# A two-layer graph kernel on one core: earlier weight sums, second-level pieces in half sets, and one block's left and right evicted whole

## The chip, the cores and the metric

The kernel runs on one core of one Trainium2 chip. A core has five engines, each with its own stream of instructions: TensorE (PE in the profile; its weight loads are PEld), VectorE (DVE), ScalarE (ACT), GpSimd (POOL) and SyncE (SP, which here only issues DMAs). An engine takes its instructions in order; semaphores tie the streams together. The metric is the device time of one execution in microseconds (us), given as the median of several runs.

## What is computed

The input `x` is 128 graphs of 64 nodes with 768 features, all in float32, and `adj` a 64 x 64 adjacency for each graph. Two layers follow each other:

```python
# layer 0: graph attention with left, self and right weights
u = softmax(h @ h.T / sqrt(d));  delta = u * adj
attn = delta / (sum(delta, 2) + 1e-10)
h_left, h_self, h_right = h @ Wl.T + bl, h @ Ws.T + bs, h @ Wr.T + br
ctx = triu(attn, 1) @ h_left + diag(attn) * h_self + tril(attn, -1) @ h_right
x = layernorm(x + relu(norm(ctx) * gamma + beta))
# layer 1: attention with 12 heads of 64
q, k, v = (x @ W + b for W, b in ((Wq, bq), (Wk, bk), (Wv, bv)))
scores = q @ k.T / 8 + abeta * adj, and -9e15 where adj <= 0
x = layernorm(x + softmax(scores) @ v)
```

## The kernel before

The 8192 rows are worked in 16 blocks of 512 rows (four tiles of 128 rows, each tile two graphs). Blocks 0 and 1 of layer 0 come before the main loop. Turn `n` of the loop then does layer 0 of block `m = n + 1` and layer 1 of block `n`, in this order on TensorE: left part, right part, own part (`self_part`) of block `m`, `values` of block `n`, and two `projected` groups (queries and keys) of block `n`. In the code the hooks of these parts are named `left`, `right`, `own`, `val`, `qk[0]` and `qk[1]`; a hook with place `k` is called ahead of product `k` of that part.

**Fewer products.** A matrix product is split into quarters and done with seven products of sums instead of eight (`seven`, `by_tokens`; `ORDER` is the order of the seven, each with two halves of the rows). An `u` eviction (L582) keeps an intermediate sum, and `last` adds the product to it on VectorE. From block `DEEP = 3` on, left and right are done together and each of the seven products is split once more into seven (`both_sides`, `nested`, 49 products); the weights of this second level lie in the DRAM tensor `lr_d`. Layer 1 does its products with fifteen sums (`products`, `FIFTEEN`).

**Weight sums.** All of these schemes need sums of weight quarters, made once. `prepare` makes the first-level sums `t5, t6, 7, t4` of a weight (tiles `b_s`, `t_s`, `b_l`, `t_l`, `b_r`, `t_r`) and stores them to `d_s`, `d_l`, `d_r`. `prepare1` makes 15 sums of the 9 raw ninths of the q, k or v weights: `loaded` issues raw loads on ScalarE's queue (L271), `summed` adds on VectorE (L304, L306), `stored` writes to `v_d` or `qk_d` from POOL's queue (L278 and after). Each raw or summed piece needs a free buffer, a "home"; homes for v are the slots of `xT` and of `x1` (`homes_of_v`). `deepened(i)` makes the second-level pieces of the left and right weights: it loads four `w_deep` tiles on SyncE's queue, copies five quarters from `d_l`/`d_r` to `lr_d`, makes eight subtractions of 128 x 192 on VectorE (L389; four for left and four for right) and stores four results (L395). The tiles `w_deep` come from the same pool of 12 buffers as the streamed weights (`wqk`, `wv`, `wlr`).

**Left and right of a block.** `ctx` needs, in one tile, the left rows of one graph above the right rows of the other (the tile `lr`, with TensorE's transposed attention beside it). Blocks 0 to 2 go by `side_part`, whose `last` evicts each bank of 128 rows in two pieces of 64 rows (L803), each to its place. Later blocks are evicted whole, and `swapped` then exchanges the wrong halves by three ScalarE copies of 64 x 768 for each of the four tiles (L854 to L856).

**What sets the order.** From L1257 on the order of instructions is the order in which the program writes them. Everything that is not a product waits in three queues, `first`, `urgent` and `lazy`; after each product `step` takes a few items from their fronts. `settle(key)` empties a queue until no item of that key is left, on the spot. So an item that is put at the front of `urgent` delays all that stands there already. `later(...)` appends; the second-level steps are put at the front:

```python
at(hooks, place + 3, lambda i=i, steps=steps: urgent.extendleft([(("d", i), *f) for f in reversed(steps)]))
```

Layer 1's softmax for head group `m` of block `n` is begun by `scores(n, m)`, which queues in `urgent`: two `largest` (L1056), two `lowered` (the maximum subtracted, L1060), `exponentials` on ScalarE (16 instructions, L1077), several gaps, and two `turn` (32 x 32 transposes on VectorE, L1081). `weighted(n, m)` calls `settle` for them and then multiplies by `v` (L1107). In turn 1, `scores(0, 1)` is hooked at left 1 and `weighted(0, 1)` at right 2.

Of the kernel before, what the change touches and what calls it, by code (L numbers as in the profile page):

```python
# [11 lines left out]
F32 = mybir.dt.float32  # L12
AF = mybir.ActivationFunctionType
ALU = mybir.AluOpType
# [3 lines left out]
P = 128  # L18
B, L, D = 128, 64, 768
# [4 lines left out]
T = 4  # L24
# [46 lines left out]
def gnn_two_layers(ctx: ExitStack, tc, x, adj, wl, bl, ws, bs, wr, br, gamma, beta,  # L71
# [36 lines left out]

    bias_lr = const.tile([P, 2, D], F32, tag="bias_lr", name="bias_lr")
    bias["l"], bias["r"] = bias_lr[:, 0, :], bias_lr[:, 1, :]  # L110
    bias["q"], bias["k"] = column(bq, "bq"), column(bk, "bk")
    abeta_c = const.tile([P, 1], F32, tag="abeta", name="abeta")
    nc.scalar.dma_start(out=abeta_c, in_=abeta.partition_broadcast(P))
    nc.vector.tensor_scalar(abeta_c, abeta_c, SCALE, None, ALU.mult)

    ident = const.tile([P, P], F32, tag="ident", name="ident")
    make_identity(nc, ident)
# [121 lines left out]
    def homes_of_v():  # L239

        xT = tp.tile([P, KC, NTOK], F32, tag="xT", name="h_v")
        yield from (xT[:, c, :] for c in range(KC))
        for t in range(T):
            yield x1_p.tile([P, D], F32, tag="x1", name="h_v")[:, 0 : 2 * TH]
# [124 lines left out]
              *[idle] * waits[2], partial(formed, 4, t4, b[1, 0], t6), queue=queue)  # L369
        return {i: a[0] for i, a in in_sbuf.items()}  # L370

    def deepened(i):


        w = {}

        def begin():
            for j, nm in enumerate("lr"):
                src = pieces[nm][i]
                for k in range(2):  # L380
                    w[j, k] = weight("w_deep").rearrange("p (h c) -> p h c", h=2)
                    nc.sync.dma_start(out=w[j, k], in_=src[:, k, :].rearrange("p (h c) -> p h c", h=2))
                nc.gpsimd.dma_start(out=lr_d[i - 1, 0:3, :, j, :].rearrange("m p c -> p m c"), in_=src[:, :, 0:QUAD])
                nc.gpsimd.dma_start(out=lr_d[i - 1, 3:5, :, j, :].rearrange("m p c -> p m c"), in_=src[:, 1:3, QUAD:HALF])

        def formed(j):
            b11, b12, b21, b22 = (w[j, k][:, h, :] for k in range(2) for h in range(2))
            for out, a, b in ((b11, b12, b11), (b12, b22, b12), (b22, b22, b11), (b21, b21, b22)):
                nc.vector.tensor_tensor(out, a, b, ALU.subtract)  # L389

        def end():
            for j in range(2):
                for k in range(2):
                    d = lr_d[i - 1, 5 + 2 * k : 7 + 2 * k, :, j, :].rearrange("m p c -> p m c")
                    nc.gpsimd.dma_start(out=d, in_=w[j, k])  # L395

        return begin, [(partial(formed, 0),), (partial(formed, 1),), (end, "gap")]

    def transposed(src, xT, t):

# [281 lines left out]
    def loads(n):  # L682

        blocks[n]["xa"] = xa = [xa_p.tile([P, D], F32, tag="xa", name=f"xa_{n}_{t}") for t in range(T)]
        return [partial(nc.sync.dma_start, out=xa[t], in_=x_t[n, t]) for t in range(T)]

    def edges(n):
        blk = blocks[n] = {}
# [91 lines left out]
    class Pairs:  # L780
# [4 lines left out]
        def __getitem__(self, t):  # L785
            if t // 2 not in self.tiles:
                self.tiles[t // 2] = l0t.tile([P, 2, 2, D], F32, tag="lr", name=f"lr_{self.n}_{t // 2}")
            return self.tiles[t // 2][:, t % 2]

    def side_part(n, nm, in_sbuf, hooks={}):  # L790


        blk = blocks[n]
        if nm == "l":
            blk["lr"] = Pairs(n)
        lr = blk["lr"]

        def last(t, h, ps, part):
            cols = slice(h * HALF, (h + 1) * HALF)
            for g in range(2):  # L800
                rows = slice(g * L, (g + 1) * L)
                half = "lr".index(nm)
                recent["u"] = nc.vector.tensor_tensor(lr[t][half * L : (half + 1) * L, g, cols], ps[rows],  # L803
                                                       bias[nm][rows, cols] if part is None else part[rows], ALU.add)

        by_tokens(nm, blk["S"], last, in_sbuf, hooks)

    def both_sides(n, hooks):
# [42 lines left out]
        def swapped(t):  # L851
            low, high = lr[t][0:L, 1, :], lr[t][L:P, 0, :]
            swap = l1s_p.tile([P, T * 6 * L], F32, tag="s", name="swap")
            nc.scalar.copy(swap[0:L, 0:D], high)  # L854
            nc.scalar.copy(high, low)
            nc.scalar.copy(low, swap[0:L, 0:D])  # L856

        return [partial(swapped, t) for t in range(T)]

    def context0(n):  # L860

# [325 lines left out]
    def now(fs):  # L1187
        for f in fs:
            f()

    edges(0)
    homes = [(-1, home) for home in homes_of_v()]
    now(loads(0))
    blocks[0]["rows"] = blocks[0]["xa"]
    in_sbuf = prepare("s", prep, prep)
    bias["s"] = row(bs, "bs")
# [62 lines left out]
    for n in range(NBLK):  # L1259
# [33 lines left out]
        if not last:  # L1293
            if n > 0:
# [229 lines left out]
```

## Time and profile before

| what | us |
|---|---|
| median of 3 runs | 2813.65 |
| the three runs | 2813.05, 2813.65, 2816.16 |
| the profiled execution, whole time | 2813.63 |
| its span in the profile | 2811.9 |
| TensorE busy | 2775.8 |
| VectorE busy | 1951.1 |
| ScalarE busy | 1099.0 |
| POOL busy | 961.5 |

The span runs from the first to the last instruction that the profile shows; some 1.7 us of the time lie around it. Rows of the time line give start, duration, engine, line, operation, output and inputs with their shape, the number of instructions that were merged, and in square brackets the idle time before the row with the one that ended it. Rows of the windows give, for each engine, busy time and instruction count, and at the end the granted TensorE clock (1.00 is full), the share of time in which the DMA engines were busy, and GB/s. Wait rows give the total, the number of times, and the longest.

The stages that the change touches lie in the first 500 us: blocks 0 and 1 until about 207 us, turn 0 of the loop until about 290 us, and turn 1 with block 2's left part from 290, its right part until about 352, its own part until about 382, then values, queries and keys.

### The profile page before, as it was taken

To read this page: it belongs to the slowest core of one execution; us is meant where nothing else is said; L and a number is where in the kernel's file an instruction comes from. 1 tells how busy PE (TensorE), PEld (TensorE's weight loads), DVE (VectorE), ACT (ScalarE), POOL (GpSimd) and SP (SyncE) were. 2 spreads that over 40 slices of the span, in tenths; PEclk is the share of its full clock that TensorE was granted. 3 is DMA by queue.
4 is the path that set the end of the run, shared out by engine and by line. 5 is a ranking of instruction groups with operands and counts; after the bars stand their busy time and mean duration, and the time that the engine had idled before them with its cause. 6 is when DMAs were issued, how large, how long until landed. Compare 5 with 4: busy or idle time off the path is not lost.

```text
span 2811.9 us, 49390 instructions
## 1 busy us (share of the span) xinstructions
PE 2775.8 (99%) x17962; PEld 2014.2 (72%) x17962; DVE 1951.1 (69%) x3412; ACT 1099.0 (39%) x1894; POOL 961.5 (34%) x1251
## 2 busy tenths in 40 slices
PE   8999999999999999999999999999999999999997
PEld 5558677586776867768577685867768677686786
DVE  5787768676685766767677676776767667676666
ACT  0013324335343453434525344353434534345253
POOL 3242234505134151442415225061341513424122
PEclk9999999999999999999999999999999999999999
DMA  9686788857759587695866858678695876948543
GB/s 339 201 294 200 210 259 268 263 157 238 219 181 271 151 258 196 190 269 152 264 184 210 249 169 265 161 230 230 184 262 152 253 204 190 269 147 260 175 128 102
DMA packets 394848, 604.88 MB, mean 215 GB/s; under 512 B 49296, under 2 KB 277648, under 8 KB 394608
## 3 DMA queue, kind: packets, MB, share of 16 engines
q1 hardware_dynamic: 337280, 495.72, 59.3%
q0 software_dynamic: 18704, 76.89, 7.7%
q10 hardware_dynamic: 38624, 29.11, 5.1%
q8 instruction: 146, 2.39, 0.4%
q14 instruction: 94, 0.77, 0.1%
HBM read 530.00 MB, written 78.45 MB: 216 GB/s over the span
## 4 chain that ended last, share of the span: by engine, by line
PE 92%; issue 2%; DMA 2%; DVE 2%; ACT 1%; POOL 0%; SPq 0%; POOLq 0%; ACTq 0%; DVEq 0%
PE ps_X L487 25%; PE ps_Y L487 17%; PE ps_Y L832 13%; PE ps_X L832 11%; PE ps_X L549 10%; PE ps_Y L549 8%; PE ps_ctx L882 3%; PE sc L1044 2%; PE ps_y L1107 2%; PE u L710 1%; PE ps_X L595 1%; ACT eT L1077 1%; DMA b_r<-in_L_gnn_W_right_dram 1%; DMA qk_d<-h_qk 0%; DVE lr L803 0%
## 5 line engine op out<-in xcount | busy, mean ns | idle before, releaser
L435 POOL TENSOR_TENSOR sums<-hT 128x768 f32<-128x768 f32 x16 | 29.7, 1855 | 794.0 <-PE ps_X L487 713.9
L1077 ACT ACTIVATE eT<-s 32x384 f32<-32x384 f32 x512 | 267.1, 522 | 13.8 <-DVE s L1060 7.4
L487 PE MATMUL ps_X<-xT,wqk 128*128 128x256 f32 x1024 | 234.2, 379 | 0.4 <-ACT xT L405 0.4
L893 ACT ACTIVATE unused<-o 128x768 f32<-128x768 f32 x60 | 50.7, 845 | 447.6 <-DMA sq<-in_x_dram 281.2
L617 DVE TENSOR_TENSOR lr<-ps_Y,u_deep 128x384 f32<-128x384 f32 x273 | 151.9, 556 | 94.8 <-PE ps_Y L832 77.0
L1020 ACT ACTIVATE qk<-ps_X,bq 128x256 f32<-128x256 f32 x128 | 60.8, 475 | 395.0 <-PE ps_X L487 394.8
L487 PEld LDWEIGHTS ps_X<-xT,wqk 128*128 128x128 f32 x1024 | 194.5, 190 | 27.0 <-ACT xT L405 0.6
L832 PE MATMUL ps_Y<-wlr,q 128*128 128x384 f32 x546 | 208.5, 491 | 0.0
L1023 DVE TENSOR_TENSOR qk<-qk,ps_X 128x512 f32<-128x512 f32 x160 | 109.7, 686 | 132.1 <-PE ps_X L487 66.9
L1118 POOL TENSOR_TENSOR o<-o,share 128x192 f32<-128x192 f32 x240 | 135.6, 592 | 146.5 <-DVE share L1115 146.4
L487 PE MATMUL ps_Y<-more,wqk 128*128 128x256 f32 x768 | 181.6, 379 | 2.4 <-DMA wqk<-qk_d 1.3
L487 PE MATMUL ps_X<-sums,wqk 128*128 128x256 f32 x768 | 180.3, 381 | 1.1 <-DVE qk L1023 1.1
L465 POOL TENSOR_TENSOR more<-xT 128x512 f32<-128x512 f32 x32 | 40.1, 1273 | 376.9 <-DVE xT L423 198.3
L487 PEld LDWEIGHTS ps_Y<-more,wqk 128*128 128x128 f32 x768 | 145.8, 190 | 22.9 <-DVE d L740 1.7
L487 PEld LDWEIGHTS ps_X<-sums,wqk 128*128 128x128 f32 x768 | 144.6, 190 | 21.5 <-DVE qk L1023 1.5
L1023 DVE TENSOR_TENSOR qk<-qk,ps_Y 128x512 f32<-128x512 f32 x160 | 108.5, 678 | 70.6 <-PE ps_Y L487 68.7
L617 DVE TENSOR_TENSOR u_deep<-ps_X,lr 128x384 f32<-128x384 f32 x195 | 107.8, 553 | 67.0 <-PE ps_X L832 57.9
L549 PE MATMUL ps_X<-ws,hT 128*128 128x384 f32 x462 | 154.0, 486 | 0.0
L832 PE MATMUL ps_X<-wlr,q 128*128 128x384 f32 x364 | 149.2, 492 | 2.3 <-issue 2.3
L832 PEld LDWEIGHTS ps_Y<-wlr,q 128*128 128x128 f32 x546 | 101.5, 190 | 67.3 <-DVE lr L617 0.2
L1158 ACT ACTIVATE unused<-o 128x768 f32<-128x768 f32 x56 | 47.4, 846 | 236.6 <-POOL o L1118 234.0
L549 PEld LDWEIGHTS ps_X<-ws,hT 128*128 128x128 f32 x462 | 87.7, 190 | 61.0 <-DMA ws<-d_s 0.2
(272 smaller groups left out, 6337.4 us busy)
## 6 DMA issues: line engine op xcount, KB each, us to landing
wlr<-lr_d SPq DMA_DIRECT2D x819, 192.0 KB, 3.6
wqk<-qk_d SPq DMA_DIRECT2D x480, 256.0 KB, 2.7
wv<-v_d SPq DMA_DIRECT2D x240, 256.0 KB, 6.1
ws<-d_s SPq DMA_DIRECT2D x180, 192.0 KB, 6.9
ws<-in_L_gnn_W_self_dram SPq DMA_DIRECT2D x135, 192.0 KB, 4.0
xa<-in_x_dram SPq DMA_DIRECT2D x64, 384.0 KB, 5.6
out_dram<-o POOLq DMA_DIRECT2D x60, 384.0 KB, 7.9
sq<-in_x_dram ACTq DMA_DIRECT2D x56, 384.0 KB, 9.3
```

The lines of the kernel that those rows point to most:

```text
L487: nc.tensor.matmul(ps[:, h, :], lhsT=a, rhs=b, start=start and h == 0 and k == 0, stop=k == len(fs[h]) - 1, skip_group_check=True)
L549: nc.tensor.matmul(ps, lhsT=a, rhs=b, start=(c == 0 and i in (1, 2, 5)), stop=(c == len(fs) - 1), skip_group_check=True)
L617: nc.vector.tensor_tensor(dst, view(ps), add, ALU.add)
L832: nc.tensor.matmul(ps, lhsT=a, rhs=b, start=(k == 0 and j in (1, 2, 5)), stop=(k == len(fs) - 1), skip_group_check=True)
L882: nc.tensor.matmul(ps[g * L : (g + 1) * L, 0:HALF], lhsT=blk["aT"][:, t, g * L : (g + 1) * L], rhs=blk["lr"][t][:, g, h * HALF : (h + 1) * ...
L893: nc.scalar.activation(unused(), o[t], AF.Identity, accum_out=total[:, t : t + 1])
L1020: nc.scalar.activation(dst[:, h], ps[:, h, :], AF.Identity, bias=bias["qk"[h]][:, c : c + 1], scale=float(sign))
L1023: nc.vector.tensor_tensor(dst, dst, ps, ALU.add if sign > 0 else ALU.subtract)
L1044: nc.tensor.matmul(sc[t // 2, r][g * L : (g + 1) * L, t % 2, c, :], lhsT=q[rows, c, tok], rhs=k[rows, c, tok], start=True, stop=True)
L1077: nc.scalar.activation(e[to[0], :, to[1]], pairs[rows, :, cols], AF.Exp, scale=1.0 / SCALE)
L1107: nc.tensor.matmul(y[h, r][cols, t, c, :], lhsT=eT[rows, 2 * h + t, c, cols], rhs=by_parity[rows, 2 * h + t, 2 * c + m, g, :], start=True, ...
L1118: nc.gpsimd.tensor_tensor(res, res, share[:, t], ALU.add)
```

## The change

The adjacency of block 0 is loaded behind the four tiles of `x`, and the lines that load `bq`, `bk` and `abeta` stand further down. Three more `prep` tiles (six homes) are put at the front of the homes for the v sums. The sums of the queries begin at place 4 of block 1's own part and those of the keys at place 7 of its left part (both 9 before). `deepened` works on one side, left or right, at a time: two `w_deep` tiles, four subtractions and two stores, in 14 slots instead of seven whole sets. Block 2's left and right are evicted in whole banks of 128 rows, and `swapped` runs for its four tiles at own 1 to 4.

```diff
-    bias["q"], bias["k"] = column(bq, "bq"), column(bk, "bk")
     abeta_c = const.tile([P, 1], F32, tag="abeta", name="abeta")
-    nc.scalar.dma_start(out=abeta_c, in_=abeta.partition_broadcast(P))
-    nc.vector.tensor_scalar(abeta_c, abeta_c, SCALE, None, ALU.mult)
...
-    def deepened(i):
-        w = {}
+    def deepened(i, j):
+        w, src = {}, pieces["lr"[j]][i]
         def begin():
-            for j, nm in enumerate("lr"):
-                src = pieces[nm][i]
-                for k in range(2):
-                    w[j, k] = weight("w_deep").rearrange("p (h c) -> p h c", h=2)
-                    nc.sync.dma_start(out=w[j, k], in_=src[:, k, :].rearrange("p (h c) -> p h c", h=2))
-                nc.gpsimd.dma_start(out=lr_d[i - 1, 0:3, :, j, :].rearrange("m p c -> p m c"), in_=src[:, :, 0:QUAD])
-                nc.gpsimd.dma_start(out=lr_d[i - 1, 3:5, :, j, :].rearrange("m p c -> p m c"), in_=src[:, 1:3, QUAD:HALF])
+            for k in range(2):
+                w[k] = weight("w_deep").rearrange("p (h c) -> p h c", h=2)
+                nc.sync.dma_start(out=w[k], in_=src[:, k, :].rearrange("p (h c) -> p h c", h=2))
+            nc.gpsimd.dma_start(out=lr_d[i - 1, 0:3, :, j, :].rearrange("m p c -> p m c"), in_=src[:, :, 0:QUAD])
+            nc.gpsimd.dma_start(out=lr_d[i - 1, 3:5, :, j, :].rearrange("m p c -> p m c"), in_=src[:, 1:3, QUAD:HALF])
...
-        return begin, [(partial(formed, 0),), (partial(formed, 1),), (end, "gap")]
+        return begin, [(formed,), (end, "gap")]
...
         def last(t, h, ps, part):
             cols = slice(h * HALF, (h + 1) * HALF)
+            if n > 1:
+                recent["u"] = nc.vector.tensor_tensor(lr[t][:, "lr".index(nm), cols], ps,
+                                                      bias[nm][:, cols] if part is None else part, ALU.add)
+                return
             for g in range(2):
...
-    edges(0)
     homes = [(-1, home) for home in homes_of_v()]
+    blocks[0] = {}
     now(loads(0))
+    edges(0)
...
     sides(0)
+    bias["q"], bias["k"] = column(bq, "bq"), column(bk, "bk")
+    nc.scalar.dma_start(out=abeta_c, in_=abeta.partition_broadcast(P))
+    nc.vector.tensor_scalar(abeta_c, abeta_c, SCALE, None, ALU.mult)
     affine_of["gamma"] = row(gamma, "gamma")
     affine_of["beta"] = row(beta, "beta")
     bias["v"] = row(bv, "bv")
+    for _ in range(3):
+        free = prep.tile([P, HC, HALF], F32, tag="w", name="h_v").rearrange("p k c -> p (k c)")
+        homes[0:0] = [(-1, free[:, k * 2 * TH : (k + 1) * 2 * TH]) for k in range(2)]
     prepare1("v", homes)
...
-    self_part(1, None, {9: [partial(prepare1, "q", homes, queue=urgent)]})
-    side_part(1, "l", None, {9: [partial(prepare1, "k", homes, queue=urgent)]})
+    self_part(1, None, {4: [partial(prepare1, "q", homes, queue=urgent)]})
+    side_part(1, "l", None, {7: [partial(prepare1, "k", homes, queue=urgent)]})
...
-        for i, (when, hooks, place) in zip(ORDER2, ((0, val, 2), (0, qk[0], 5), (1, left, 8), (1, own, 3),
-                                                    (1, qk[0], 0), (1, qk[0], 7), (1, qk[1], 3))):
+        slots = ((0, val, 2), (0, val, 7), (0, qk[0], 0), (0, qk[0], 4), (0, qk[0], 8), (0, qk[0], 12), (0, qk[1], 2),
+                 (1, left, 1), (1, left, 4), (1, left, 7), (1, left, 10), (1, qk[0], 0), (1, qk[0], 3), (1, qk[0], 6))
+        for k, (when, hooks, place) in enumerate(slots):
             if when == n:
-                begin, steps = deepened(i)
+                i, j = ORDER2[k // 2], k % 2
+                begin, steps = deepened(i, j)
                 at(hooks, place, begin)
-                at(hooks, place + 3, lambda i=i, steps=steps: urgent.extendleft([(("d", i), *f) for f in reversed(steps)]))
+                more_at = (qk[1], 0) if hooks is qk[0] and place == 12 else (hooks, place + 3)
+                at(*more_at, lambda i=i, steps=steps: urgent.extendleft([(("d", i), *f) for f in reversed(steps)]))
...
                     side_part(m, "l", None, left)
                     side_part(m, "r", None, right)
+                    for t in range(T):
+                        at(own, 1 + t, swapped, blocks[m]["lr"], t)
```

`swapped` is moved out of `both_sides` unchanged, with the tile as an argument.

More of the change, by code (lines that the diff above doesn't have):

```diff
@@ L370, in prepare, with formed @@
         return {i: a[0] for i, a in in_sbuf.items()}
-    def deepened(i):
-        w = {}
+    def deepened(i, j):
+        w, src = {}, pieces["lr"[j]][i]
         def begin():
-            for j, nm in enumerate("lr"):
-                src = pieces[nm][i]
-                for k in range(2):
-                    w[j, k] = weight("w_deep").rearrange("p (h c) -> p h c", h=2)
-                    nc.sync.dma_start(out=w[j, k], in_=src[:, k, :].rearrange("p (h c) -> p h c", h=2))
-                nc.gpsimd.dma_start(out=lr_d[i - 1, 0:3, :, j, :].rearrange("m p c -> p m c"), in_=src[:, :, 0:QUAD])
-                nc.gpsimd.dma_start(out=lr_d[i - 1, 3:5, :, j, :].rearrange("m p c -> p m c"), in_=src[:, 1:3, QUAD:HALF])
-        def formed(j):
-            b11, b12, b21, b22 = (w[j, k][:, h, :] for k in range(2) for h in range(2))
+            for k in range(2):
[3 more added lines that the diff above has]
+            nc.gpsimd.dma_start(out=lr_d[i - 1, 3:5, :, j, :].rearrange("m p c -> p m c"), in_=src[:, 1:3, QUAD:HALF])
+        def formed():
+            b11, b12, b21, b22 = (w[k][:, h, :] for k in range(2) for h in range(2))
             for out, a, b in ((b11, b12, b11), (b12, b22, b12), (b22, b22, b11), (b21, b21, b22)):
@@ L391, in end @@
         def end():
[L392 to L395, printed above, removed]
-        return begin, [(partial(formed, 0),), (partial(formed, 1),), (end, "gap")]
+            for k in range(2):
+                d = lr_d[i - 1, 5 + 2 * k : 7 + 2 * k, :, j, :].rearrange("m p c -> p m c")
+                nc.gpsimd.dma_start(out=d, in_=w[k])
+        return begin, [(formed,), (end, "gap")]
     def transposed(src, xT, t):
@@ L687, in edges @@
     def edges(n):
-        blk = blocks[n] = {}
+        blk = blocks.setdefault(n, {})
         blk["at"] = tmp.tile([P, T, L], F32, tag="adj", name=f"adj_{n}", bufs=3)
@@ L788, in __getitem__, with swapped @@
             return self.tiles[t // 2][:, t % 2]
+    def swapped(lr, t):
+        low, high = lr[t][0:L, 1, :], lr[t][L:P, 0, :]
+        swap = l1s_p.tile([P, T * 6 * L], F32, tag="s", name="swap")
+        nc.scalar.copy(swap[0:L, 0:D], high)
+        nc.scalar.copy(high, low)
+        nc.scalar.copy(low, swap[0:L, 0:D])
     def side_part(n, nm, in_sbuf, hooks={}):
@@ L849, in both_sides @@
                lambda b: bias_lr[:, :, HALF + b * QUAD : HALF + (b + 1) * QUAD], hooks)
[L851 to L858, printed above, removed]
+        return [partial(swapped, lr, t) for t in range(T)]
     def context0(n):
@@ L1189, in now @@
             f()
+    homes = [(-1, home) for home in homes_of_v()]
+    blocks[0] = {}
+    now(loads(0))
     edges(0)
-    homes = [(-1, home) for home in homes_of_v()]
-    now(loads(0))
     blocks[0]["rows"] = blocks[0]["xa"]
```

## The prediction

> **What bounds the kernel now.** I read the page's busy shares, then TensorE's waits, then the time lines of VectorE and ScalarE around each wait, and last the windows with the granted clock.
>
> ```profile
> span 2811.9 us, 49390 instructions
> PE 2775.8 (99%) x17962; PEld 2014.2 (72%) x17962; DVE 1951.1 (69%) x3412; ACT 1099.0 (39%) x1894; POOL 961.5 (34%) x1251
> ...
> PE ps_x L404 <- DMA xa<-in_x_dram: 5.4, 1, 5.4
> PE ps_Y L549 <- DVE lr L803: 3.9, 2, 3.1
> PE ps_X L832 <- issue: 2.3, 1, 2.3
> PE ps_y L1107 <- DVE eT L1081: 1.5, 1, 1.5
> PE sc L1044 <- DVE qk L1023: 1.4, 1, 1.4
> ...
> PE ps_X L487 <- issue: 1.3, 1, 1.3
> PE ps_Y L487 <- DMA wqk<-qk_d: 1.3, 1, 1.3
> ```
>
> TensorE (PE) is busy 99% of the span, so only its idle time can be won, and a new wait of TensorE is lost whole. The wait rows give us in total, times, longest. The matmuls stand in the same order in both built programs, and from about 500 us on the other engines' orders are the same too. There TensorE is busy without a gap until the tail. So the time changes by TensorE's idle time before 500 us, and by the clock after it. Inside that stretch idle is 5.39 at the start, 3.09 at 55.8, about 0.8 near 105, 0.59 and 0.78 at 172 and 177, 1.53 at 325, and 1.30, 1.28, 1.40 and 2.25 at 404, 433, 472 and 478.
>
> **Part 1, loads at the start.** Behind the four x loads, the adjacency load lets the first x land 0.49 us sooner (one issue on the SyncE queue). At 22.60 TensorE takes the first matmul of `t_s,sums`, whose POOL sums hang on the third b_s load (landing at 14.82), not on x, so the half microsecond is waited back. The bq, bk and abeta lines move in the text only: on ScalarE's queue they stay the first three. I take 0 (0 to -0.5).
>
> **Part 2, free homes for the v sums.** Two instead of five raw v loads are issued in the first 20 us, and two stores leave 24 to 27 us: 5 x 256 KB = 1.28 MB less. The wait that this meets:
>
> ```profile
> 57.04 0.56 DVE L355 TENSOR_TENSOR t_r<-b_r 128x384 f32<-128x384 f32 x1 [7.81 <-DMA b_r<-in_L_gnn_W_right_dram]
> 57.63 1.12 DVE L803 TENSOR_TENSOR lr<-ps_Y,u 64x384 f32<-64x384 f32 x2
> ...
> 58.90 3.78 PE L549 MATMUL ps_Y<-t_l,sums 128*128 128x384 f32 x6 [3.09 <-DVE lr L803]
> ...
> 56.00:57.00 1.00, 0.00 (x0) 0.00 (x0) 0.00 (x0) 0.00 (x0) 0.00 (x0) 1.00 1.10 393
> ...
> 59.00:60.00 1.00, 1.00 (x3) 0.56 (x4) 0.97 (x3) 0.00 (x0) 0.36 (x1) 0.66 1.03 389
> 60.00:61.00 1.00, 1.00 (x3) 0.58 (x2) 1.00 (x3) 0.00 (x0) 0.74 (x2) 0.50 0.59 221
> 61.00:62.00 1.00, 1.00 (x3) 0.51 (x2) 1.00 (x3) 0.00 (x0) 0.84 (x2) 0.50 0.77 287
> 62.00:63.00 1.00, 1.00 (x4) 0.56 (x3) 1.00 (x2) 0.00 (x0) 0.77 (x2) 0.64 0.58 215
> ```
>
> VectorE is held 7.81 us by a sum of the right weights, the eviction behind it is late, and TensorE stands 3.09 us. The windows end with granted clock, DMA share and GB/s: DMA is full at 393, so 1.28 MB is 1.28/0.39 = 3.3 us of it, and b_r can land at about 53.7, enough for no stall. After the stall the clock falls: (1-0.66)+0.50+0.50+(1-0.64) = 1.7 us more. The Trainium skill (TensorE: Matmul & The Clock Gate, "Part 1: The HAM clock gate") has the clock halve only after an idle window of about 3.4 us: by it this stall of 3.09 would cost 3.1, by the rows 4.8. The rows decide. (The 2.25 us stall at 478 left the clock at 1.00.) I take -4.0 of 0 to -4.8, since the b_r loads are also gated by TensorE's use of their buffers. The v loads now come when TensorE frees the t_l pieces, near 67 to 70 us, with sums from about 75 on; landings here take 7 to 12 us under full DMA, so they are just in time. Price 0 (0 to +1.5).
>
> **Part 3, q and k sums sooner.** VectorE starts on the q sums at about 134 us instead of 142, and the sums in block 1's right part (each 0.68 to 0.76, as at L306 and L304), which sat before late evictions, thin out. The 0.59 and 0.78 stalls go; VectorE stays tight (83 of 101 us busy from 105 to 206), and one of 0.7 may return. -0.7 (-1.4 to +0.7).
>
> **Part 4, half sets.** The 56 subtractions stay 56; a half set is four of them in a row, 1.45 us. In the first loop turn (207 to 290 us) there are seven half sets against two whole ones: three more, 4.4 us of VectorE beside 17 us of its idle time, and each less than the 3.45 us of two products by which an eviction must be done (a product is 3.45/2 us here): 0 (0 to +2).
>
> The harm is in block 2's left part (290 to 325 us). A half set is pushed to the front of `urgent`, at hooks 4, 7, 10 and 13, once per three products, where before one set came at hook 11. What they push back is the softmax chain of `scores(0, 1)`, in the same queue. Before it ran thus:
>
> ```profile
> 301.16 0.96 DVE L1060 TENSOR_TENSOR s<-s,mx 128x768 f32<-128x768 f32 x1
> 302.14 0.56 DVE L582 TENSOR_TENSOR u<-ps_X,bias_lr 128x384 f32<-128x384 f32 x1
> 302.62 0.95 DVE L1060 TENSOR_TENSOR s<-s,mx 128x768 f32<-128x768 f32 x1
> ...
> 325.21 0.56 DVE L582 TENSOR_TENSOR u<-ps_X,bias_lr 128x384 f32<-128x384 f32 x1 [0.59 <-PE ps_X L549]
> 325.69 1.83 DVE L1081 STREAM_TRANSPOSE eT<-eT 128x768 f32<-128x768 f32 x2
> ...
> 303.67 1.28 ACT L1077 ACT_TABLE_LOAD   x1 [8.78 <-DVE s L1060]
> 304.96 8.54 ACT L1077 ACTIVATE eT<-s 32x384 f32<-32x384 f32 x16
> ...
> 326.71 1.79 PE L1107 MATMUL ps_y<-v,eT 64*64 64x65 f32 x96 [1.53 <-DVE eT L1081]
> ```
>
> The second subtraction of the maximum (302.62) releases ScalarE, whose 16 exponentials end at 313.5, 12 us ahead of the transposes. In the changed program's VectorE order this second subtraction stands behind both u evictions of the right part's product 1 and directly before the two transposes: it is no longer popped step by step, but emptied out by `settle` when `weighted(0, 1)` is written. TensorE's order is unchanged: `weighted(0, 1)` comes at 325.18. Then: eviction 325.21, subtraction 325.69 to 326.64, table load 1.28, exponentials 8.54, first transpose half of 1.83 with 0.1 to start: 326.7 + 1.3 + 8.5 + 1.0 = 337.6 against 326.71: **+10.9 us**, with no cover: VectorE and ScalarE each take their instructions in order, and TensorE has the matmuls behind it. The Trainium skill (ScalarE: Activation LUTs, on what ACT_TABLE_LOAD costs) adds a drain of about 1.38 to the load, 2.66 in all; here the exponentials follow 0.01 us after the 1.28 load, so +10.9, where the page would give +12.3. The stall of 12.5 us also ends cold, as that at 58.9 did: +1.7, together **+12.6**.
>
> **Part 5, block 2 evicted whole.** 32 evictions of 64 rows (0.555 us each at L803) become 16 of 128 rows (0.556, the like row at L582 and L774): 16 x 0.56 = 8.9 us less on VectorE in 290 to 352. That shortens no wait but leaves room for the half sets. ScalarE gets 12 copies of 64x768, 0.83 each by its rows at L854 to L856, 10 us, in 352 to 382, where it is busy 4 of 30 us. Queued behind them are the sq loads (issued at 377.07 before): with the copies done near 368 they lose nothing: 0 (0 to +1).
>
> **Part 6, what follows the stall.** For 11 us TensorE stands while DMA and POOL go on, no set is left in block 2's own part (the 8 subtractions at 365 and their four stores), and the q and k stage of this turn has three half sets instead of three whole ones. The waits there were: sq landing late (VectorE held 4.01 until 403.41; TensorE 1.30), wqk behind the w_deep loads on SyncE (1.28), VectorE's backlog (1.40 and 2.25). All of it is 6.2; I take -4.5 (0 to -6.2).
>
> **Sum.** 0 - 4.0 - 0.7 + 0 + 12.6 + 0 - 4.5 = +3.4 us on the profiled execution, 2813.63 (span 2811.9 and 1.7 around it); the median of three runs is 2813.65, so the same: 2817.0. A measurement of this kernel can tell about 0.2%, 5.6 us, so this counts as within it, on the slow side.
>
> **Rivals.** *A, slower: b_r does not land sooner.* Place: the stall at 55.8. Its third load waits 4.9 us for TensorE and is issued at 46.2 whatever the traffic before. For it: that wait. Against: DMA is full from there to 57. Price: the 4.0 fails, +7.4, 2821.0. It decides from a landing later than 56.2 on: then over 2.25 us of idle are left, and the clock may still fall.
> *B, slower: the waits from 404 to 478 stay* (VectorE is busy 58 of 70 us from 430 to 500): the 4.5 fails, +7.9, 2821.5. With A, +11.9, 2825.5.
> *C, faster: the softmax chain is not late*, because something I have not seen lets the exponentials go early. Then -4.0 - 0.7 - 4.5 = -9.2, 2804.4. Against it is the instruction order itself.
> *D, the change does not do what it says at the start:* the ScalarE queue's order is indeed unchanged; 0.
>
> **How the numbers follow.** The forecast 0.43; A 0.24, B (with and without A) 0.18; C and the like 0.15. The range 2808 to 2826 holds the forecast and most of A and B; left out are C and a tail where all bounds are bad. Faster 0.15, same 0.43, slower 0.42.
>
> **What would show it.** TensorE's waits: `ps_y <- DVE eT` near 12.5 us once, at about 320 to 325 plus what was won, with a table load and 16 exponentials inside, and a clock under 1 after it; no wait for lr at 55.8, b_r landing by 54; none or little at 172 and 177; at most one of the four waits after 400. Wrong, if the exponentials end well ahead of the transposes, if the stall at 55.8 stays, or if a new wait over 1 us shows in 207 to 290 us.

## The result, and the profile after

The changed kernel takes 2826.22 us, the median of 5 runs (2823.75 to 2827.95), against 2816.16 for the kernel before in 5 runs beside it (2813.05 to 2818.98). The ratio is 1.0035, with a 95% interval of 1.0025 to 1.0046: slower, by 10 us. The forecast was 2817.0, in a range of 2808 to 2826, and no difference that can be told. The measured time lies on the slow side, 0.2 us beyond the range.

The page and TensorE's waits (in total, times, longest), of the changed kernel:

```profile
span 2826.2 us, 49392 instructions
PE 2778.6 (98%) x17962; PEld 2015.9 (71%) x17962; DVE 1944.2 (69%) x3396; ACT 1107.1 (39%) x1906; POOL 960.5 (34%) x1251
...
PE ps_y L1105 <- DVE eT L1079: 12.5, 1, 12.5
PE ps_x L398 <- DMA xa<-in_x_dram: 5.8, 3, 4.4
PE ps_X L543 <- DMA wl<-d_l: 2.8, 1, 2.8
PE ps_X L543 <- DVE u L576: 2.3, 2, 2.0
PE ps_Y L543 <- DVE lr L808: 1.6, 2, 0.9
```

The wait for eT of 1.5 us has become 12.5. New are a wait for a `wl` load and one for a `u` eviction; the waits of the 404 to 478 us stretch are gone from the list. The matmuls stand in the same order in all kernels of this study, 17962 of them, so the start of the k-th matmul in one profile less that in another says where time is lost or won. By stage, in us, against the profile of before:

| stage (time before) | forecast | changed kernel | the same once more (`after_again`) |
|---|---|---|---|
| start, to 28 | 0 | +2.6 | +2.7 |
| the wait at 55.8 and the clock after it | -4.0 | -5.0 | -5.0 |
| block 1, 164 to 200 | -0.7 | +3.0 | +2.4 |
| end of turn 0, 283 to 293 | 0 | +1.6 | +1.6 |
| block 2's left part, 312 to 324 | 0 | +3.0 | +2.7 |
| the softmax chain, 324 to 348 | +12.6 | +13.5 | +13.6 |
| 404 and 433 | -4.5, both rows together | -3.1 | -3.1 |
| 472 and 478 | in the row above | -3.8 | -3.8 |
| later | 0 | +1.8 | +0.6 |
| sum | +3.4 | +13.7 | +11.7 |

The two profiled executions are 14.3 us apart and the medians 10.1: the profile of before was one of its quicker executions, that of the changed kernel the slowest of its five. The experiments show which rows are the change's own and which are an execution's luck.

### The profile page after: what moved, and what is told of

It is laid out like the page before. It is cut to its first block, busy times and chain, and to the rows that moved or that the text cites. A ratio compares the mean times of both kernels' runs of the same rounds, so it can differ in the third digit from the quotient of the medians.

```text
span 2826.2 us, 49392 instructions
## 1 busy us (share of the span) xinstructions
PE 2778.6 (98%) x17962; PEld 2015.9 (71%) x17962; DVE 1944.2 (69%) x3396; ACT 1107.1 (39%) x1906; POOL 960.5 (34%) x1251
## 4 chain that ended last, share of the span: by engine, by line
PE 93%; DVE 2%; DMA 2%; ACT 2%; issue 1%; POOL 0%; ACTq 0%; SPq 0%; POOLq 0%
PE ps_X L481 25%; PE ps_Y L481 17%; PE ps_Y L837 13%; PE ps_X L837 10%; PE ps_X L543 10%; PE ps_Y L543 8%; PE ps_ctx L880 3%; PE sc L1042 2%; PE ps_y L1105 2%; PE u L704 2%; ACT eT L1075 1%; PE ps_X L589 1%; DMA bs<-in_L_gnn_b_self_dram 0%; DMA qk_d<-h_qk 0%; DVE lr L808 0%
```

## The experiments

Runs named `b_` are the kernel before with a part of the change; those named `a_` are the changed kernel with an edit.

### Parts of the change alone, on the kernel before

The adjacency behind x:

```diff
-    edges(0)
     homes = [(-1, home) for home in homes_of_v()]
+    blocks[0] = {}
     now(loads(0))
+    edges(0)
```

> The kernel before, with one edit: block 0's adjacency is loaded behind the four tiles of x. In the changed kernel TensorE's first matmul of t_s,sums comes at 25.28 us, 2.6 later than before. Theory: this edit does it (the adjacency's 256-byte rows now go beside the last x tiles and the b_s loads): t_s,sums at 24.5 to 25.5, a stretch of half clock near 11 us, and the whole 1 to 3 us longer. Rival: it comes from the other loads (fewer h_v) or from the scatter of single executions: t_s,sums within 0.5 us of 22.6.

Measured 2815.72 against 2815.07, ratio 1.0002 (0.9994 to 1.0010). The first `t_s,sums` is 1.0 later than before, with no half clock near 11 us: less than the theory had it, more than the rival allowed. In the median the edit by itself costs nothing that can be told, though the interval reaches up to 2.8 us; the theory as stated falls.

The free homes:

```diff
+    for _ in range(3):
+        free = prep.tile([P, HC, HALF], F32, tag="w", name="h_v").rearrange("p k c -> p (k c)")
+        homes[0:0] = [(-1, free[:, k * 2 * TH : (k + 1) * 2 * TH]) for k in range(2)]
     prepare1("v", homes)
```

> The kernel before, with one edit: three more prep tiles as homes for the v sums, so that two instead of five raw v loads and no v store go before 57 us. Theory: the full DMA queue is shorter and b_r lands by 54: no wait for lr at 55.8, no half clock after it, 4 to 5 us less by 62 us. Rival: b_r is held by TensorE's use of its buffers: the wait stays near 3.1. On block 1 (160 to 200 us): if the 3.0 us that the changed kernel lost there come from TensorE running ahead of the k weight's loads, they show here too; if from the sooner q and k sums, not.

Measured 2810.36, ratio 0.9983 (0.9974 to 0.9991): 4.7 us faster. Of the two time lines of VectorE below, the first is of the changed kernel, the second of this one: the first sum of the right weights no longer starts at 57.04.

```profile
54.19 0.56 DVE L352 TENSOR_TENSOR t_r<-b_r 128x384 f32<-128x384 f32 x1 [2.35 <-DMA b_r<-in_L_gnn_W_right_dram]
```

```profile
54.77 0.56 DVE L355 TENSOR_TENSOR t_r<-b_r 128x384 f32<-128x384 f32 x1 [4.48 <-DMA b_r<-in_L_gnn_W_right_dram]
```

It still waits for b_r, but the eviction behind it is in time for TensorE, and the wait of 3.09 and the half clock are gone. In the four profiles without the free homes that wait is not of one size: 3.09 (before), 3.47 (`b_start`), 1.47 (`b_sooner`) and 3.73 (`b_whole`), with half clock behind the first and the last alone. So -5.0 is what the one profile of before had to lose. In block 1 `b_homes` loses 1.0 of the changed kernel's 3.0.

The sooner q and k sums:

```diff
-    self_part(1, None, {9: [partial(prepare1, "q", homes, queue=urgent)]})
-    side_part(1, "l", None, {9: [partial(prepare1, "k", homes, queue=urgent)]})
+    self_part(1, None, {4: [partial(prepare1, "q", homes, queue=urgent)]})
+    side_part(1, "l", None, {7: [partial(prepare1, "k", homes, queue=urgent)]})
```

> The kernel before, with one edit: q sums from place 4 of block 1's own part, k sums from place 7 of its left part. Theory: this is what costs 3.0 us in block 1 of the changed kernel (VectorE waits for a raw k weight's load, 3.1 us near 166): TensorE's idle time in 160 to 200 us goes from 1.4 to 3 or more. Rival: the edit is harmless by itself and takes away the waits of 0.59 and 0.78: idle time there under 1.4.

Measured 2814.69, ratio 0.9997 (0.9989 to 1.0005). Idle time in block 1's right part is 0.66 + 0.69 + 0.89 = 2.2, between the two forecasts. A wait of 0.9 at 185 is this edit's own (every kernel with it has one of 0.88 to 0.92). But kernels without the edit lose time there too against the profile of before: `b_start` 1.4, `b_homes` 1.0, `b_whole` 1.9. Part of the 3.0 is luck of that one profile; more on this at the end of the experiments.

Block 2 evicted whole, with `swapped` at own 1 to 4:

```diff
+            if n > 1:
+                recent["u"] = nc.vector.tensor_tensor(lr[t][:, "lr".index(nm), cols], ps,
+                                                      bias[nm][:, cols] if part is None else part, ALU.add)
+                return
```

> The kernel before, with one edit: block 2's left and right evicted whole, and 12 ScalarE copies in its own part. Forecast: VectorE 9 us less busy in 290 to 352, TensorE's waits there unchanged (1.5 for eT), the sq loads on ScalarE's queue not later: 0 to 1 us by 400 us. Rival: the copies hold the sq loads, and the wait near 405 grows past 2 us.

Run once, 2815.19; the wait for eT is 1.6, and from 200 to 400 us it loses 0.5. As forecast, it costs and brings next to nothing by itself, as far as one execution tells.

### The chain of scores(0, 1)

First the whole of the stall in the changed kernel, from the time lines of VectorE, ScalarE and TensorE:

```profile
330.50 0.56 DVE L576 TENSOR_TENSOR u<-ps_X,bias_lr 128x384 f32<-128x384 f32 x1 [1.38 <-PE ps_X L543]
330.98 0.95 DVE L1058 TENSOR_TENSOR s<-s,mx 128x768 f32<-128x768 f32 x1
341.86 1.84 DVE L1079 STREAM_TRANSPOSE eT<-eT 128x768 f32<-128x768 f32 x2 [9.94 <-ACT eT L1075]
...
325.36 3.78 ACT L929 ACTIVATE o<-o,c,rstd 128x768 f32<-128x768 f32 x4 [31.15 <-DVE c L925]
332.03 1.28 ACT L1075 ACT_TABLE_LOAD   x1 [2.89 <-DVE s L1058]
333.32 8.51 ACT L1075 ACTIVATE eT<-s 32x384 f32<-32x384 f32 x16
...
342.99 2.88 PE L1105 MATMUL ps_y<-v,eT 64*64 64x65 f32 x96 [12.52 <-DVE eT L1079]
```

It is the forecast row by row: the subtraction between the second eviction and the transposes, then 1.28 and 8.51. But ScalarE shows one thing more: four normalisations of block 1 (L929) now stand ahead of the exponentials, held until 325.36 by a factor that VectorE computes late (at 325.18; at 315.74 in `a_slots` below, where two of the half sets stand elsewhere). The test is to put half sets behind the `lowered` only:

```diff
-                at(*more_at, lambda i=i, steps=steps: urgent.extendleft([(("d", i), *f) for f in reversed(steps)]))
+                def more(i=i, steps=steps):
+                    k = 0
+                    while k < len(urgent) and getattr(urgent[k][1], "func", gap).__name__ in ("largest", "lowered"):
+                        k += 1
+                    for f in reversed(steps):
+                        urgent.insert(k, (("d", i), *f))
+
+                at(*more_at, more)
```

> The changed kernel, with one edit: a half set is put behind the two maximum subtractions (lowered) of a softmax chain where these stand at the front of the urgent queue, not ahead of them. VectorE's second subtraction for scores(0, 1) comes back to where it was. Theory: the wait of 12.5 us for eT falls to under 2 and the half clock after it goes: 12 to 13.5 us less near 327 to 350. What follows tells two readings apart: if TensorE's standstill gave the later stages their room, the waits of 1.3, 1.3, 1.4 and 2.3 at 405 to 478 return (whole: about 6 us under the changed kernel); if moving the sets out of block 2's own part did it, they stay away (whole: 12 to 13 us under it, some 2814 or less). A half set now comes later, so w_deep buffers are held longer: the wait for wl at 316 may grow by up to 2 us.

Measured 2822.55, ratio to before 1.0025 (1.0017 to 1.0032). The wait for eT is still 8.7. `lowered` is back at 306.68, and yet on ScalarE's time line:

```profile
327.12 3.78 ACT L929 ACTIVATE o<-o,c,rstd 128x768 f32<-128x768 f32 x4 [30.70 <-DVE c L925]
330.92 1.28 ACT L1075 ACT_TABLE_LOAD   x1
332.22 8.51 ACT L1075 ACTIVATE eT<-s 32x384 f32<-32x384 f32 x16
```

The expectation of under 2 fails: the late subtraction was one of two causes in a row. The exponentials themselves are items of the queue, and half sets ahead of them put them behind the normalisations. (At the end of turn 0 this rule loses 2.7 instead of 1.6.) So they go ahead as well:

```diff
-... in ("largest", "lowered"):
+... in ("largest", "lowered", "exponentials"):
```

> The changed kernel, with half sets put behind the leading lowered and exponentials of a softmax chain in the urgent queue, not ahead of them. With the lowered alone ahead, the exponentials still began only at 330.9, behind four normalisations of block 1 that waited on ScalarE for a VectorE factor until 327. Theory: ScalarE's order is the second half of the cause; with the exponentials ahead too, the wait for eT is under 2 us, as before the change. Rival: w_deep or wl transfers, later by the half set that is pushed back, hold TensorE instead; then 2 us or more of waits for wl in 312 to 328.

Run once, 2814.95: eT 3.1, and waits for `wl` and `wr` of 0.75, 0.52, 0.16 and 0.84, 2.3 together. The theory's "under 2" fails by the subtractions of one half set, which now stand directly before the transposes (329.96 to 331.49 on VectorE); the exponentials themselves are done at 313.98. The rival held as well: the chain is repaired, and weight loads are late instead, by what seems to be the half set that is pushed back and holds its buffers longer. In turn 0 this rule takes away the waits at 283 to 293 entirely (0 against +1.6). Last, the queue as in the change, but the sets elsewhere:

```diff
-                 (1, left, 1), (1, left, 4), (1, left, 7), (1, left, 10), (1, qk[0], 0), ...
+                 (1, left, 7), (1, left, 10), (1, own, 2), (1, own, 5), (1, qk[0], 0), ...
```

> The changed kernel, with the four half sets of block 2's left part put elsewhere: from left 1, 4, 7, 10 to left 7, left 10, own 2, own 5. The second lowered of scores(0, 1) and its exponentials then stand where they stood before the change, on VectorE and on ScalarE. Theory (the chain was late because half sets took its turns in the queue, on both engines): the wait for eT is 1.5 us, no half clock after it, and the whole 12 to 16 us under the changed kernel, 2810 to 2814. Whether the waits of 1.4 and 2.3 at 472 and 478 stay away tells where their gain came from: the standstill of 12.5 us (then they are back, 3.7 us) or the sets that left the last two stages of this turn (then not).

Measured 2814.57, ratio 0.9998 (0.9989 to 1.0007), some 12 us under the changed kernel, and just above the 2810 to 2814 expected. ScalarE and TensorE:

```profile
302.10 1.28 ACT L1075 ACT_TABLE_LOAD   x1 [11.42 <-PE ps_y L1105]
303.39 8.52 ACT L1075 ACTIVATE eT<-s 32x384 f32<-32x384 f32 x16
...
325.52 1.79 PE L1105 MATMUL ps_y<-v,eT 64*64 64x65 f32 x96 [1.62 <-DVE eT L1079]
```

The exponentials end at 311.9, some 13 us ahead of TensorE's need. The wait for `wl` is gone too, and 472 and 478 still cost 3.7 less than before though TensorE stood nowhere: that gain comes from the sets that left the second turn's last stages, not from the standstill.

The wait for `wl` in the changed kernel, on TensorE, and behind it what SyncE's queue waited for in 300 to 330 us:

```profile
318.80 1.56 PE L543 MATMUL ps_X<-wl,hT 128*128 128x384 f32 x4 [2.75 <-DMA wl<-d_l]
...
SPq L570 <- DMA lr_d<-w_deep: 5.4, 4, 2.2
```

Four times a weight load stood still until a half set's result had been stored from the buffer that it needs. With the four half sets as in the change TensorE's wait is 1.9 to 2.8 in three profiles; with two of them (`a_slots`, `best_a`, `best_b` below) or three (`best_c` to `best_e`) it is 0. So their number and place in the left part decide. The queue's waits alone do not: in `a_slots` there are still 5.7 us of them, three times, and TensorE loses nothing. How far the loads run ahead of TensorE was not varied by itself.

### The start

> The changed kernel, with block 0's adjacency loaded first again, ahead of x. Each edit alone (adjacency behind x; fewer early v loads) moved TensorE's first t_s,sums by about 1 us, together by 2.6 to 4.3, where the second t_s sum on VectorE began at 18.2 behind a late b_s load and ran for 4.5 us beside two POOL sums (1.36 us alone). Theory: both are needed to bring b_s late enough; with the adjacency first the sum runs ahead of POOL's at 1.4 us, and t_s,sums is at 22.6 to 24. Rival: the fewer v loads alone do it with the other edits: still at 25 or later.

The edit is that of `b_start` undone. Run once, 2820.40; `t_s,sums` is 1.0 later than before, and the chain as in the changed kernel (12.5). That is in keeping with the theory. The other side of it:

> The kernel before, with the adjacency behind x and the free homes for the v sums, nothing else. In the changed kernel and two of its three variants with both edits the first t_s,sums came at 24.9 to 25.3, in one at 22.5; with one or none of the edits at 22.6 to 24. Theory: the two together make it a race between the second t_s sum and POOL's sums, lost in most executions: some 2 us slower in the median than the free homes alone (2810.4), 2811.5 to 2814. Rival: the start varies from run to run and no edit matters: 2810 to 2811.

Measured 2813.46 (2808.6 to 2819.0), ratio 0.9994 (0.9987 to 1.0001): 3.1 slower than the free homes alone. But its one profile shows the quick start, and at 404 and 433 it loses 4.5 more than theirs: the median cannot be booked on the start.

> The changed kernel once more, beside the others on one chip: 2823 to 2829; a wait of 12.5 us for eT, 2 to 3 us for wl near 315 to 319, none at 472 and 478. If the start is a race, t_s,sums is again near 25 or near 22.5, and nothing between; the 404 and 433 waits, which came and went with no edit near them, may show.

Measured 2825.57, ratio 1.0036 (1.0022 to 1.0049); `t_s,sums` at 25.37. VectorE, then POOL, then TensorE, of this run:

```profile
15.65 1.36 DVE L354 TENSOR_TENSOR t_s<-b_s 128x1152 f32<-128x1152 f32 x1 [4.25 <-DMA b_s<-in_L_gnn_W_self_dram]
18.27 4.55 DVE L354 TENSOR_TENSOR t_s<-b_s,t_s 128x1152 f32<-128x1152 f32 x1 [1.26 <-DMA b_s<-in_L_gnn_W_self_dram]
...
18.02 1.82 POOL L430 TENSOR_TENSOR hT<-hT 128x768 f32<-128x768 f32 x1
19.79 1.81 POOL L441 TENSOR_TENSOR sums<-hT,sums 128x768 f32<-128x768 f32 x1
...
25.37 4.11 PE L543 MATMUL ps_X<-t_s,sums 128*128 128x384 f32 x12 [2.26 <-DVE u L576]
```

and of `a_slots`, whose start has the same edits:

```profile
16.61 1.36 DVE L354 TENSOR_TENSOR t_s<-b_s,t_s 128x1152 f32<-128x1152 f32 x1
...
17.60 2.04 POOL L430 TENSOR_TENSOR hT<-hT 128x768 f32<-128x768 f32 x1
```

If the last b_s quarter lands in time, the second sum is all but done when POOL begins (1.36). If not, it begins beside POOL's two sums and takes 4.55, and the `u` eviction behind it is late: 2.0 to 3.3 us of TensorE, in four of the six profiles of kernels with both edits, in none of the eleven others. The changed kernel and `a_slots` have the same start and differ in this, so it is a race. What makes it losable shows on SyncE's queue, here of before and of the changed kernel:

```profile
3.74 4.17 SPq L233 DMA_DIRECT2D b_s<-in_L_gnn_W_self_dram  x4
...
4.66 5.03 SPq L230 DMA_DIRECT2D b_s<-in_L_gnn_W_self_dram  x4
```

The last of the four b_s loads is issued at 7.2 to 7.8 us in the ten profiles with the adjacency first, and at 8.6 to 9.7 in the seven with it behind x. It lands at 16.15 to 17.09 in the ten, and at 18.05 to 18.19 in the four that lose, while POOL begins at 17.55 to 18.02. So in these profiles it takes the adjacency behind x to lose. Whether the free homes are needed too is not shown: with the adjacency behind x and without them there is one profile (`b_start`), and it won, but so did that of `b_both`.

### Better versions, and the wait at 404

`best_a` is the changed kernel with the adjacency first, the places of `a_slots` and the rule of `a_chain2`; `best_b` leaves out the sooner sums and the whole eviction as well.

> The changed kernel with three edits together: the adjacency first again, the left part's half sets at left 7, left 10, own 2, own 5, and half sets put behind a chain's lowered and exponentials where these stand at the front. Forecast, stage by stage against the kernel before: start 0 to +1, the wait at 55.8 gone (-5), block 1 as before within 1, no wait at 283 to 293, 1.6 for eT at 325, no waits at 472 and 478 (-3.8): about -8, 2805 to 2809. If the -3.8 was bought with the standstill, it is missing here: 2809 to 2812.

> As the version before it, but with the q and k sums at their old places and block 2 evicted in halves, so that only the free homes and the half sets are left of the change. If these two parts are worth nothing by themselves, it is equal to that version within 2 us; if the room on VectorE in block 2 (9 us) or the sooner sums carry part of the gain, it is 2 us or more slower, with waits for lr in 172 to 190 or in 300 to 350.

Measured 2811.65, ratio 0.9985 (0.9979 to 0.9992), and 2810.76, 0.9981 (0.9974 to 0.9988). They are equal within 2 us, as expected, but both some 4 to 5 us short of a forecast of about 2807. `best_a` fell into the range set out for the case that the 3.8 us at 472 and 478 had been bought with the standstill, but by chance: its profile keeps them (-3.7). What is missing lies at 404, where TensorE waited 4.3 and 3.4 us with half clock after it. VectorE and TensorE of `best_b`:

```profile
395.26 0.69 DVE L987 TENSOR_TENSOR v<-v,ps_Y 128x512 f32<-128x512 f32 x1
402.01 1.08 DVE L417 STREAM_TRANSPOSE hT<-sq 128x512 f32<-128x512 f32 x1 [6.07 <-DMA sq<-in_x_dram]
...
403.76 3.51 PE L481 MATMUL ps_X<-wv,more 128*128 128x256 f32 x8 [3.37 <-issue]
```

Two kernels take the sets out of that stretch: `best_c` on `best_b`, `best_d` on `best_a`.

```diff
+        slots = ((0, val, 2), (0, val, 7), (0, val, 11), (0, qk[0], 0), (0, qk[0], 4), (0, qk[0], 8), (0, qk[0], 12),
+                 (0, qk[1], 2), (1, left, 4), (1, left, 7), (1, left, 10), (1, qk[0], 3), (1, qk[0], 6), (1, qk[0], 9))
```

> The free homes and the half sets alone (q and k sums and block 2's eviction as before the change, adjacency first), half sets behind a chain's lowered and exponentials, and other places: eight of them in the first loop turn (val 2, 7, 11; qk0 0, 4, 8, 12; qk1 2), three at left 4, 7, 10 of the second, three at qk0 3, 6, 9, none in block 2's own part. Open is what the wait near 404 is (nothing in some runs, 2.2 to 4.3 and half clock in others, in all variants whose TensorE did not stand at 325). Theory: the sq tile's loads land behind the sets' own DMA of 352 to 400; with none there the wait is gone: 404 to 440 free of waits, whole 2806 to 2809. Rival: the full DMA there is the streamed ws, wv and out traffic; the wait stays at 2 to 4, whole 2810 to 2812. Bounds: three half sets in the left part may bring back 0.5 to 1.5 us of waits for wl, and eight in the first turn 1 us at 283 to 293.

> The same places for the half sets, with the sooner q and k sums and block 2 evicted whole. Against the version before it this tells what those two are worth once the half sets harm nothing: by the runs so far nothing within 1 us, with a wait of 0.9 at 185 from the sooner sums and 9 us less of VectorE in block 2. If the theory on the 404 wait holds, 2806 to 2809 as well.

Measured 2808.10, ratio 0.9970 (0.9958 to 0.9982), and 2806.43, 0.9963 (0.9950 to 0.9975). In both profiles there is no wait from 330 to 460 us; VectorE of `best_d`:

```profile
398.90 0.69 DVE L991 TENSOR_TENSOR v<-v,ps_Y 128x512 f32<-128x512 f32 x1
399.50 1.10 DVE L417 STREAM_TRANSPOSE hT<-sq 128x512 f32<-128x512 f32 x1
```

The tile lands before it is asked for: the sets in block 2's own part were the cause. In all eight profiles without sets there, the changed kernel's included, there is no wait at 404; six of the nine with sets there have one, of 1.3 to 4.3 us. The theory's mechanism, the sets' DMA making the sq loads land late, is the smaller part. Counted from the same matmul, the one at 352.1 us in the profile of before, the last of the four loads is issued at 34.9 to 37.1 us without sets and at 38.3 to 42.7 with them; to its landing it takes 9.1 to 10.7 us and 10.4 to 12.9. The loads start late more than they are slow: the first waits for VectorE's transposes out of the same tile (21.8 to 21.9 us against 25.0 to 27.3). Whether VectorE's steps or the DMA of the sets cause that is not separated.

`best_d` is 9 us faster than the kernel before it was run beside, and some 20 faster than the change. It also shows what the whole eviction is good for: with three half sets in the left part, VectorE in `best_c` is late with eT (2.8 and half clock, 2.2 more than in `best_d`), with the 9 us of room it is not.

The last kernel is `best_d` with the q and k sums at place 9 again, as before the change.

> The quickest version so far (best_d) with the q and k sums back at their old places. Over all profiles, kernels without the sooner sums lose 0.8 us in block 1 in the mean against the profile of before (7 profiles, -0.1 to 1.9), kernels with them 2.0 (9 profiles, 1.1 to 3.1). Theory: the sooner sums cost about 1.2 us, by a wait of 0.9 at 185: without them no wait there, and the whole 0.5 to 2 us under best_d, 2804.5 to 2806. Rival: the difference is an execution's luck: within 0.5 us of best_d, and the waits near 170 and 175 grow instead.

Measured 2806.72, ratio 0.9966 (0.9952 to 0.9980), where `best_d` had 0.9963 (0.9950 to 0.9975). In block 1 it loses 1.4 against 3.1 in `best_d`, the wait at 185 is gone, and waits of 0.9, 0.9 and 0.8 stand at 166, 169 and 174. Over all profiles the stage loses 0.9 in the mean without the sooner sums (8 profiles) and 2.0 with them (9), so about 1 us is likely the edit's own; the timed runs can't tell it from 0, and neither theory is shown.

## Why the prediction was right or wrong

**Part 4, the chain, was right**: 12.5 us of wait forecast, 12.5 measured, for the cause named. Its clock term was small: 1.7 forecast, 2.5 measured. The subtraction was only the first of two late steps, which the forecast of its size didn't need and a repair did. Rival C is out.

**Part 2 was right**: b_r lands by 54.19 (forecast "about 53.7"), -5.0 instead of -4.0 (just past its bound of -4.8), and rival A is out. The rows decided rightly against the page's 3.4 us: in the profile of before the half clock did follow that stall. It need not have: in `b_start` the wait is 3.47 and no half clock follows.

**The steps that failed are those costed at nothing.** Part 1: "the half microsecond is waited back" took the landing of the b_s loads as fixed. x does come 0.96 us sooner, but the last b_s load is issued 1.9 us later and slips behind the start of POOL's sums, and the sum on VectorE takes 4.46 us instead of 1.36: +2.6. Part 4, turn 0: "less than the 3.45 us of two products" holds for one half set against one eviction, not for a row of them with softmax steps: +1.6, inside its bounds of 0 to +2; with the rule of `a_chain2`, which lets the softmax steps go first, it is 0. Part 4, block 2: nothing was said of the buffers. The text costed the subtractions on VectorE and left out that each half set takes two weight buffers until POOL has stored them (eight in the left part, where the one whole set before took four), and that SyncE's loads stand behind that: +3.0. Together these are 7.2 of the 10.3 us by which the profile differs from the sum.

**Part 3** (-0.7, measured +3.0): the 0.59 and 0.78 of one profile were taken as the stage's cost and as won; kernels that don't touch the stage lose up to 1.9 more there. The edit itself brings a wait of 0.9; its net cost, about 1 us over all profiles, is not shown by the timed runs.

**Part 5** was right: 0.

**Part 6** (-4.5, measured -6.9) was right in sign and in two of its three reasons. The standstill of TensorE, the first, is not needed: `best_d` has none and shows -3.0 and -3.8 in these rows all the same. Fewer sets in the q and k stage take away the waits at 433, 472 and 478 in all eleven profiles that have only half sets there (rival B is out), and no sets in block 2's own part take away the one at 404. The size was too low: -4.5 of the 6.2 that stood there, where all of it went. How much there was to win at 404 and 433 is luck: the profile of before had lost 2.6 there, and `b_homes`, with the same code there, 0.2.

## What to carry to other kernels

In a kernel that is bound by one engine, a step that is put at the front of a shared queue is priced by what it pushes back, on each engine in turn: here 6 us of subtractions moved 10 us of exponentials onto the path, and moving one link of that chain forward only uncovered the next. A cost of zero needs in it the buffers, the loads that an edit moves back in their queue, and what an instruction costs beside another engine, not only the count of instructions. And one profile's small waits are a sample: a kernel that leaves a stage alone is the control for it, and the k-th matmul's start in both gives the difference at once.

## What the runs showed of the hardware

A VectorE sum of two 128x1152 tiles took 1.34 to 1.36 us alone. Begun beside POOL's two sums it took 2.6, and POOL's then 2.0 and 2.9 instead of 1.8; or 4.2 to 4.6, and POOL's 1.8 each. Which of the two gives way differs from case to case. In the rows of `after_again` above, VectorE's sum ends 1.22 us after POOL's second, though alone it takes 1.36: beside POOL it got almost nowhere. In these of before it is POOL's second sum that ends 1.68 us after VectorE's, with 1.8 to do:

```profile
19.02 2.63 DVE L357 TENSOR_TENSOR t_s<-b_s,t_s 128x1152 f32<-128x1152 f32 x1
...
18.40 2.04 POOL L436 TENSOR_TENSOR hT<-hT 128x768 f32<-128x768 f32 x1
20.40 2.93 POOL L447 TENSOR_TENSOR sums<-hT,sums 128x768 f32<-128x768 f32 x1
```

The clock after a wait is a matter of phase. Waits of 2.23 and 2.25 us (`b_both`, `b_sooner`) were followed by 3.4 us of half clock, waits of 2.25, 2.49 and 3.47 (before, `a_slots`, `b_start`) were not. In the changed kernel the granted clock changes at 10.82, 14.23, 335.08 and 348.74 us, which lie 1, 94 and 4 times 3.413 us apart, and the other profiles have such a grid too. That fits a window that runs free of the waits, as the Trainium skill (TensorE: Matmul & The Clock Gate, "Part 1: The HAM clock gate") has it. But the page's idle window of about 3.4 us need not be wholly idle here. Between 20 and 500 us of all 17 profiles, at full clock, the half clock came behind each stretch of this grid that was idle for 62% or more (62% in `best_c`, of a wait of 2.76), and behind none idle for 58% or less (58% in the changed kernel, of the wait of 2.75 at 318.80). The wait of 3.47 in `b_start` lies across two stretches, with 50 and 52%.

After the wait of 12.5 the half clock outlasted the restart at 342.99 by 5.7 us; the windows, with the clock third from the end:

```profile
343.00:344.00 1.00, 1.00 (x37) 1.00 (x41) 0.70 (x1) 0.00 (x0) 0.00 (x0) 0.50 0.00 0
...
347.00:348.00 1.00, 1.00 (x3) 0.46 (x2) 0.00 (x0) 0.00 (x0) 0.00 (x0) 0.50 0.00 0
348.00:349.00 1.00, 1.00 (x4) 0.56 (x3) 0.00 (x0) 0.00 (x0) 0.00 (x0) 0.63 0.00 0
349.00:350.00 1.00, 1.00 (x5) 0.60 (x4) 0.52 (x2) 0.00 (x0) 0.00 (x0) 1.00 0.00 0
```

The prediction took 1.7 us from the stall of 3.09; this one cost 2.5. The length of the wait is not the reason: in `a_edges`, after the same 12.52 us and a restart at 338.97, full clock was back 2.6 us later, and the half clock cost 1.0. There the stretch of the grid in which TensorE restarted was idle for 23%, and the next one had full clock; here it was idle for 32%, and the next one had not. The windows of `a_edges`:

```profile
341.00:342.00 1.00, 1.00 (x33) 0.93 (x28) 0.00 (x0) 0.00 (x0) 0.00 (x0) 0.70 0.00 0
342.00:343.00 1.00, 1.00 (x4) 0.59 (x4) 0.00 (x0) 0.00 (x0) 0.00 (x0) 1.00 0.00 0
```
